# Local attention: queries and keys projected with features on partitions, instead of tokens and transposes

## The chip, the cores and the metric

The kernel runs on one core of a Trainium2 chip. The metric is the device time of one execution in microseconds; lower is better. The page of the profile and the trace come from one profiled execution. The engines are TensorE (PE, with PEld for its weight loads), VectorE (DVE), ScalarE (ACT), GpSimd (POOL) and SyncE (SP), which only issues transfers here. ACT and POOL have DMA queues of their own too.

## The reference

Input `x` is (4, 512, 256) in f32: four batches of 512 tokens. Three stages come first and are not touched by the change: a mixture of experts, a block attention with feature maps, and a second attention with a field term. Then two layers of a local transformer follow, each with its own weights:

```python
def _layer(x, wqkv, qs, ksc, wo, lg, lb, w1, b1, w2, b2):
    h = shift_token(x)                  # half of the features come from the token before
    q, k, v = jnp.split(h @ wqkv, 3, axis=-1)       # 8 heads of 64 each
    q = l2norm(q) * qs
    k = l2norm(k) * ksc
    q, k = rotary_xpos(q, k)
    ...                                 # local attention, @ wo, residual, feed forward

def l2norm(t):
    return t / jnp.clip(jnp.linalg.norm(t, axis=-1, keepdims=True), 1e-12)

def rotate_half(x):
    x1, x2 = jnp.split(x, 2, axis=-1)
    return jnp.concatenate([-x2, x1], axis=-1)

# in rotary_xpos:
q = q * cos * scale + rotate_half(q) * sin * scale
k = k * cos / scale + rotate_half(k) * sin / scale
```

Local attention has windows of 128 tokens: a query sees the keys of its own window and of the one before, up to 128 back, with a factor of 8 on the products. A key tile of 128 therefore meets 256 queries (128 at the end of the sequence). The feed forward normalizes, projects to twice 682 features, gates with gelu and projects back.

## The kernel before

The whole local transformer is in `local_stream`. `y[b]` holds a batch with tokens on partitions. The work of one layer is built of pieces for each batch.

`front(w, b, d)` makes queries, keys and values. It turns `y[b]` into `yT` with features on partitions (eight transposes into `pdt`, two copies). For each of four token tiles and each of queries and keys, `project` runs two 128x512 products with the tokens stationary, so that the result has tokens on partitions and all eight heads along its rows. ScalarE squares it (L614), VectorE sums the squares of each head (L615), multiplies by the table `tab` (L617) and multiplies the swapped halves by the second part of the table (L621, two instructions), and GpSimd adds the two (L624) into `qr`. A swap of halves is only another view along the row there. After all four tiles come a square root, a maximum and a reciprocal on the lengths `ss` (L628 to L630) and four value projections with copies (L633). Then the queries are multiplied by their lengths (L639), and 32 transposes into `pqt` (L82, through the helper) with copies (L646) give `qT` and `kT`, features on partitions. `mm` records every product at L78.

`scores(d, c, u)` takes a pair of heads `c` and a half `u` of the key tiles: products into `pds` with keys on partitions, Exp (L666, one instruction for each key tile, with the key's length as the scale), and a product with the mask `lmask` (L668). `values(l, b, d, c)` multiplies by the values (`pn`), and for every second `c` sums the exponentials with `ones32` (`pz`); the sums go through memory (SP's transfers L698 to L705: `sums`, `rden`, `rows`, `zb`) and come back spread over partitions for the product at L708. `tail` is the output projection `pdy`, `normed`, `turned`, `hidden` and `output` the feed forward; `turned` adds the last bias on GpSimd (L751).

What runs in which order on TensorE is written out by hand: inside `PE.in_order()` the products keep the order of the program. The loop over `k` goes through batches and head pairs; between `scores` and `values` it calls `spend`, which takes steps of a filler, `beside(b)`: steps of the next batch's `front`, then of the `tail` of the batch before.

```python
if b < B:
    scores(ds[b], c, 0)
spend(2 if b < B - 1 else 1)
if k > 0:
    b0, c0 = divmod(k - 1, 4)
    values(l, b0, ds[b0], c0)
spend(2 if b < B - 1 else 1)
if b < B:
    scores(ds[b], c, 1)
spend(2 if b < B - 1 else 1)
```

`first_two` prepares the fronts of batches 0 and 1 (`lead` runs ahead of the loop; in layer 1 it runs beside the end of layer 0's feed forward). The last batch's filler is the feed forward. The other engines' order comes from a scheduler that follows the program. The pool `lp` holds two buffers of a tag where nothing else is said; the feed forward's `u` tiles use the tags `kT` and `qT`.

Of the kernel before, what the change touches and what calls it, by code (L numbers as in the profile page):

```python
# [63 lines left out]
def adaln_attn_ffn_kernel(ctx: ExitStack, tc: tile.TileContext, a: dict, out: bass.AP):  # L64
# [115 lines left out]
    def row(name):  # L180
        return rows[name]
# [381 lines left out]
    def local_stream(dw, lp, y, dr):  # L563
        ones32 = dw.tile([128, 32], F32, tag="ones32", name="ones32")
        nc.gpsimd.memset(ones32, 1.0)

        def attn_weights(l):
            wqkv = weight("wqkv", [128, 2, 3 * DIN], a["f_wqkv"][l].rearrange("(c p) o -> p c o", p=128), dw)
            wo = weight("wo", [128, 4, H], a["f_wo"][l].rearrange("(c p) o -> p c o", p=128), dw)

            tab = weight("tab", [128, 4, NT, DHD], a["rot"], dw)
            for s, nm in enumerate(("qs", "ks")):
                sc = row(nm)[:, l * DHD : (l + 1) * DHD]
                nc.vector.tensor_tensor(
                    tab[:, 2 * s], tab[:, 2 * s], sc.unsqueeze(1).to_broadcast([128, NT, DHD]), ALU.mult)
                for d0, d1 in ((0, 32), (32, 0)):
                    nc.vector.tensor_tensor(
                        tab[:, 2 * s + 1, :, d0 : d0 + 32], tab[:, 2 * s + 1, :, d0 : d0 + 32],
                        sc[:, d1 : d1 + 32].unsqueeze(1).to_broadcast([128, NT, 32]), ALU.mult)
            return SimpleNamespace(wqkv=wqkv, wo=wo, tab=tab)  # L580

        def ffn_weights():
            return SimpleNamespace(w1=dw.tile([128, 2, 2 * HIDW], F32, tag="w1", name="w1"),
                                   w2=dw.tile([128, NU + 1, H], F32, tag="w2", name="w2"))

        def load_ffn(l, w):
            load(w.w1, a["f_w1"][l].rearrange("(c p) o -> p c o", p=128))
            load(w.w2, a["f_w2"][l].rearrange("(c p) o -> p c o", p=128))

        def front(w, b, d):  # L590

            yT = lp.tile([128, 2, S + 1], F32, tag="yT", name="yT", bufs=1)
            nc.gpsimd.memset(yT[:, 1, 0:1], 0.0)
            for c in range(2):
                pt = mmt("pdt")
                for k in range(NT):
                    PE.transpose(pt[:, k * 128 : (k + 1) * 128], y[b][:, k, c * 128 : (c + 1) * 128], ident)
                nc.scalar.copy(yT[:, c, 1 : S + 1], pt)
                yield

            def project(t, s):
                lhs = [yT[:, 0, 1 + t * 128 : 1 + (t + 1) * 128], yT[:, 1, t * 128 : (t + 1) * 128]]
                ps = mmt("pdq")
                mm(ps, [(lhs[c], w.wqkv[:, c, s * DIN : (s + 1) * DIN]) for c in range(2)])
                return ps.rearrange("p (h d) -> p h d", d=DHD)

            d.ss = ss = lp.tile([128, NT, 2, DH], F32, tag="ss", name="ss")
            qr = []
            for t in range(NT):
                qr_t = lp.tile([128, 2, DH, DHD], F32, tag="qr", name="qr", bufs=4)  # L610
                for s in range(2):
                    p3 = project(t, s)
                    sq = lp.tile([128, DH, DHD], F32, tag="tmp", name="sq", bufs=3)
                    nc.scalar.activation(sq, p3, AF.Square)  # L614
                    nc.vector.reduce_sum(ss[:, t, s, :], sq, axis=AX.X)  # L615
                    t1 = lp.tile([128, DH, DHD], F32, tag="t1", name="t1")
                    nc.vector.tensor_tensor(  # L617
                        t1, p3, w.tab[:, 2 * s, t, :].unsqueeze(1).to_broadcast([128, DH, DHD]), ALU.mult)
                    t2 = lp.tile([128, DH, DHD], F32, tag="tmp", name="t2", bufs=3)
                    for d0, d1 in ((0, 32), (32, 0)):  # L620
                        nc.vector.tensor_tensor(  # L621
                            t2[:, :, d0 : d0 + 32], p3[:, :, d1 : d1 + 32],
                            w.tab[:, 2 * s + 1, t, d0 : d0 + 32].unsqueeze(1).to_broadcast([128, DH, 32]), ALU.mult)
                    nc.gpsimd.tensor_tensor(qr_t[:, s], t1, t2, ALU.add)  # L624
                    yield
                qr.append(qr_t)

            nc.scalar.activation(ss, ss, AF.Sqrt)  # L628
            nc.vector.tensor_scalar_max(ss, ss, 1e-12)
            nc.vector.reciprocal(ss, ss)  # L630
            d.v = lp.tile([128, NT, DH, DHD], F32, tag="v", name="v")
            for t in range(NT):
                nc.scalar.copy(d.v[:, t], project(t, 2))  # L633
                yield

            d.kT = lp.tile([128, 4, S], F32, tag="kT", name="kT")
            d.qT = lp.tile([128, 4, S], F32, tag="qT", name="qT")
            for t in range(NT):
                nc.vector.tensor_tensor(  # L639
                    qr[t][:, 0], qr[t][:, 0], ss[:, t, 0].unsqueeze(2).to_broadcast([128, DH, DHD]), ALU.mult)  # L640
                for s, dst in enumerate((d.qT, d.kT)):
                    pt = mmt("pqt")
                    for c in range(4):
                        PE.transpose(pt[:, c * 128 : (c + 1) * 128],
                                     qr[t][:, s, 2 * c : 2 * c + 2, :].rearrange("p h d -> p (h d)"), ident)
                    nc.scalar.copy(dst[:, :, t * 128 : (t + 1) * 128], pt.rearrange("p (c q) -> p c q", q=128))  # L646
                    yield
# [3 lines left out]
        def scores(d, c, u):  # L651
            pss = [mmt("pds") for r in range(2)]
            n = 512 - 128 * u
            for jj in range(2):
                j = 2 * u + jj
                e = min((j + 2) * 128, S)
                for r in range(2):
                    rr = slice(64 * r, 64 * r + 64)
                    PE.matmul(pss[r][:, jj * 256 : jj * 256 + e - j * 128],
                              d.kT[rr, c, j * 128 : (j + 1) * 128], d.qT[rr, c, j * 128 : e],  # L660
                              start=True, stop=True)
            for r in range(2):
                p = lp.tile([128, n], F32, tag=f"p{u}", name="p", bufs=5)
                for jj in range(2):
                    at = slice(jj * 256, min(jj * 256 + 256, n))
                    nc.scalar.activation(p[:, at], pss[r][:, at], AF.Exp,  # L666
                                         scale=d.ss[:, 2 * u + jj, 1, 2 * c + r : 2 * c + r + 1])
                nc.vector.tensor_tensor(p[:, :n], p[:, :n], lmask[:, :n], ALU.mult)  # L668
                d.ps[c, u, r] = p
# [15 lines left out]
        def values(l, b, d, c):  # L685
# [17 lines left out]
            zb = lp.tile([128, 2, S], F32, tag="zb", name="zb", bufs=1)  # L703
# [37 lines left out]
        def turned(l, b, f):  # L741
            f.hT = lp.tile([128, 2, S], F32, tag="hT", name="hT")
            for c in range(2):
# [8 lines left out]
                y[b], y[b], row("fb2")[:, l * H : (l + 1) * H].unsqueeze(1).to_broadcast([128, NT, H]), ALU.add)  # L752
# [54 lines left out]
        def feed_forward(l, w):  # L807
# [3 lines left out]
            yield from turned(l, 0, fs[0])  # L811
            for b in range(B):
                for i, _ in enumerate(hidden(l, w, fs[b])):
                    yield b
                    if i == 0 and b + 1 < B:
                        normed(b + 1, fs[b + 1])
                if b + 1 < B:
                    yield from turned(l, b + 1, fs[b + 1])
                yield from output(l, w, b, fs[b])


        load_rows("drows", dw)
        lmask = dw.tile([128, 4 * WIN], F32, tag="lmask", name="lmask")
        nc.scalar.dma_start(lmask, a["kmask"])
        wf = ffn_weights()
# [6 lines left out]
        def first_two(w, ds):  # L832
            first, second = (front(w, b, ds[b]) for b in range(2))

            def lead():
                for _ in range(20):
                    next(first)
                    yield
                for _ in range(2):
                    next(second)  # L840
                    yield
                yield from first
# [4 lines left out]
        with PE.in_order():  # L847
            for l in range(2):
# [4 lines left out]
                def beside(b):  # L853
# [8 lines left out]
                    for _ in range(9 if b else 7):  # L862
# [11 lines left out]

                for k in range(4 * B + 1):
# [6 lines left out]
                    spend(2 if b < B - 1 else 1)  # L882
# [3 lines left out]
                    spend(2 if b < B - 1 else 1)  # L886
                    if b < B:
                        scores(ds[b], c, 1)
                    spend(2 if b < B - 1 else 1)
# [833 lines left out]
def _shape_constants():  # L1723
# [35 lines left out]
    for sc in (f(8.0) * scale, f(1.0) / scale):  # L1759
        c, s = cos * sc, sin * sc  # L1760
        parts += [np.concatenate([c, c], 1), np.concatenate([-s, s], 1)]
    rot = np.stack(parts).astype(f).reshape(4, NT, 128, DHD).transpose(2, 0, 1, 3)
    return {"mconst": mconst, "bmask": bmask, "hmask": hmask, "lmask": lmask, "kmask": kmask, "peT": peT, "rot": rot}
# [3 lines left out]
def _lay_out(n):  # L1767
# [6 lines left out]
    def rows_of(w):  # L1774
# [24 lines left out]

    cols = {  # L1800
# [22 lines left out]
        "f_w1": fw1.reshape(2, H, 2 * HIDW), "f_w2": fw2,  # L1823
# [21 lines left out]
```

## Time and profile before

| what | value |
|---|---|
| three runs | 1388.95, 1391.64, 1391.56 us; median 1391.56 |
| profiled execution | 1386.44 us, span 1384.7 us |
| mean granted TensorE clock | 0.991 |
| busy: PE, DVE, ACT, POOL | 1335.9, 653.3, 587.7, 232.8 us |
| local transformer, in the span | about 722 to 1384 us |
| transposes into `pqt` | 256, 33.9 us busy |
| `project` and value products | 384 records, 177.1 us busy |

The time of the profiled execution is its span and 1.7 us around it. Groups of instructions go by line, engine, operation and tile; after the bar come busy microseconds, mean nanoseconds of one, and the engine's idle time just ahead of them with what ended it. A f32 product shows as two records, a transpose as one. Windows give busy time of each engine in a stretch, and the granted clock.

### The profile page before, as it was taken

The page shows a single profiled execution, that of the slowest core. Times are in us where ns is not written, and L with a number is a line of the kernel's source. Part 1 is how long each engine was busy: PE and PEld are TensorE (multiplying, and loading weights), DVE is VectorE, ACT ScalarE, POOL GpSimd, SP SyncE. Part 2 cuts the span into 40 slices and gives each one's busy share as a digit, 9 for nine tenths or more (in the row PEclk, how much of TensorE's full clock was granted, in tenths as well). Part 3 has the DMA queues.
Part 4 walks back from the last instruction along what each step waited for, and adds up shares of the span by engine and source line. Part 5 has one row for each costly group of instructions (what it writes and reads, how often), then busy time and mean ns, then how long its engine had stood idle before and what let it go on. Part 6 is the DMA issues. An engine that isn't in the chain of part 4 may idle for free.

```text
span 1384.7 us, 19465 instructions
## 1 busy us (share of the span) xinstructions
PE 1335.9 (96%) x7632; PEld 827.5 (60%) x7632; DVE 653.3 (47%) x1295; ACT 587.7 (42%) x997; POOL 232.8 (17%) x223
## 2 busy tenths in 40 slices
PE   5999999998999999999999999999999999999998
PEld 4788888874566633333334555656555566556654
DVE  6222212224777643332227687654362777854421
ACT  4111111125555355454655756662223667474111
POOL 1325322211000011010104232100020322310110
PEclk7999999999999999999999999999999999999999
DMA  4577667633000000000210001210001010011000
GB/s 143 209 261 271 226 218 250 208 121 126 1 1 1 1 1 1 1 1 1 88 53 21 17 25 32 78 40 24 23 1 42 24 33 25 17 40 41 22 24 25
DMA packets 43085, 94.74 MB, mean 68 GB/s; under 512 B 9568, under 2 KB 25064, under 8 KB 40168
## 3 DMA queue, kind: packets, MB, share of 16 engines
q1 hardware_dynamic: 37560, 81.81, 17.8%
q0 software_dynamic: 3792, 10.24, 2.2%
q10 hardware_dynamic: 1632, 1.34, 0.3%
q8 instruction: 63, 1.03, 0.3%
q14 instruction: 38, 0.31, 0.1%
HBM read 84.08 MB, written 7.21 MB: 66 GB/s over the span
## 4 chain that ended last, share of the span: by engine, by line
PE 89%; DVE 5%; ACT 2%; DMA 2%; issue 1%; SPq 0%; DVEq 0%; POOLq 0%; POOL 0%; ACTq 0%
PE ph L78 14%; PE pdq L78 12%; PE pfy L78 6%; PE pug L78 5%; PE pv L78 5%; PE pua L78 5%; PE sc L78 5%; PE po L78 4%; PE pn L78 4%; PE pdy L78 4%; PE pds L78 4%; PE pz L78 2%; PE pqt L82 2%; PE pqk L78 1%; PE pf L78 1%
## 5 line engine op out<-in xcount | busy, mean ns | idle before, releaser
L78 PE MATMUL pdq<-wqkv,yT 128*128 128x512 f32 x384 | 177.1, 602 | 0.0
L416 ACT ACTIVATE cex<-sc 128x1024 f32<-128x1024 f32 x128 | 124.0, 1021 | 96.7 <-PE sc L78 95.9
L78 PE MATMUL ph<-h,w 128*128 128x256 f32 (+1 forms) x704 | 133.4, 347 | 0.5 <-ACT h L1398 0.5
L624 POOL TENSOR_TENSOR qr<-t,t 128x512 f32<-128x512 f32 x64 | 85.9, 1343 | 266.4 <-DVE t L621 221.7
L668 DVE TENSOR_TENSOR p<-p,lmask 128x384 f32<-128x384 f32 (+1 forms) x128 | 92.4, 736 | 68.4 <-ACT p L666 67.2
L78 PEld LDWEIGHTS ph<-h,w 128*128 128x128 f32 x704 | 116.1, 191 | 12.9 <-ACT h L1398 0.7
L78 PEld LDWEIGHTS pdq<-wqkv,yT 128*128 128x128 f32 x384 | 69.6, 190 | 78.1 <-issue 72.8
L1398 ACT ACTIVATE h<-ph,w 128x256 f32<-128x256 f32 (+1 forms) x88 | 35.4, 438 | 182.7 <-PE ph L78 130.1
L1400 DVE TENSOR_SCALAR h<-ph,w 128x256 f32<-128x256 f32 (+1 forms) x88 | 36.1, 438 | 162.4 <-PE ph L78 109.2
L666 ACT ACTIVATE p<-pds,ss 128x256 f32<-128x256 f32 (+1 forms) x256 | 96.1, 457 | 39.1 <-PE pds L78 30.6
L78 PE MATMUL pug<-hT,w 128*128 128x512 f32 x160 | 76.8, 602 | 0.0
L78 PE MATMUL sc<-qm,kT 32*128 32x512 f32 x512 | 75.2, 639 | 0.2 <-ACT cex L416 0.2
L78 PE MATMUL pua<-hT,w 128*128 128x512 f32 x160 | 75.2, 592 | 0.0
L614 ACT ACTIVATE sq<-pdq 128x512 f32<-128x512 f32 x64 | 38.3, 598 | 85.2 <-PE pdq L78 49.2
L78 PE MATMUL pv<-cex,v 128*32 128x512 f32 x512 | 69.0, 604 | 2.1 <-DVE xT L290 2.1
L78 PE MATMUL ph<-xbT,w 128*128 128x256 f32 (+1 forms) x352 | 68.5, 347 | 0.5 <-ACT xbT L123 0.5
L387 POOL TENSOR_SCALAR fterm<-vw,faT 128x256 f32<-128x256 f32 x16 | 14.6, 925 | 320.3 <-DVE cr L377 320.3
L78 PE MATMUL po<-w,h 128*128 128x256 f32 x296 | 67.7, 380 | 0.5 <-ACT h L1398 0.5
L78 PE MATMUL pds<-qT,kT 64*128 64x256 f32 (+1 forms) x512 | 65.3, 375 | 0.0
L78 PEld LDWEIGHTS pds<-qT,kT 64*128 64x128 f32 x512 | 43.9, 186 | 32.9 <-issue 25.8
L78 PEld LDWEIGHTS ph<-xbT,w 128*128 128x128 f32 x352 | 58.4, 191 | 7.7 <-issue 0.9
L78 PE MATMUL pdy<-wo,oT 128*128 128x256 f32 x256 | 61.5, 386 | 0.0
(301 smaller groups left out, 2129.9 us busy)
## 6 DMA issues: line engine op xcount, KB each, us to landing
w<-in_moe_w_dram SPq DMA_DIRECT2D x22, 1024.0 KB, 6.3
w<-in_moe_w_dram SPq DMA_DIRECT2D x22, 640.0 KB
w<-in_moe_w_dram SPq DMA_DIRECT2D x22, 516.0 KB, 3.8
zb<-rows SPq DMA_DIRECT2D x32, 256.0 KB, 4.0
g<-ys SPq DMA_DIRECT2D x6, 512.0 KB, 5.1
wqkv<-in_f_wqkv_dram SPq DMA_DIRECT2D x2, 1536.0 KB
w<-in_f_w_dram SPq DMA_DIRECT2D x2, 1408.0 KB, 6.1
out_dram<-yc SPq DMA_DIRECT2D x16, 128.0 KB, 1.8
```

Of the source, the lines that this page charges most:

```text
L78: cls._queue(nc.tensor.matmul(*args, **kw))
L82: cls._queue(nc.tensor.transpose(*args, **kw))
L387: nc.gpsimd.tensor_scalar_mul(fterm[:, t, :], vw, W["faT"][:, t, b : b + 1])
L416: nc.scalar.activation(ex, pss[j], AF.Exp, scale=CHD**-0.5)
L614: nc.scalar.activation(sq, p3, AF.Square)
L624: nc.gpsimd.tensor_tensor(qr_t[:, s], t1, t2, ALU.add)
L666: nc.scalar.activation(p[:, at], pss[r][:, at], AF.Exp, scale=d.ss[:, 2 * u + jj, 1, 2 * c + r : 2 * c + r + 1])
L668: nc.vector.tensor_tensor(p[:, :n], p[:, :n], lmask[:, :n], ALU.mult)
L1398: nc.scalar.activation(dst, src, AF.Relu, bias=bias)
L1400: nc.vector.tensor_scalar(dst, src, bias, 0.0, ALU.add, ALU.max)
```

## The change

Queries and keys are now projected with the weight slice stationary and `yT` moving, so that the products come out with features on partitions, two heads of 64 to each 128 (`piece`). Copies put them straight into `qT` and `kT`. The rotation's partner of a feature is now on another partition: for each two pieces four transfers on SP's queue copy 32 partitions each (128 KB) into `sw`. The q and k scales are a column (`qks`) in two three-operand products with a table that has features on partitions (`tab`, loaded once from `rotT`), and GpSimd adds in place. Lengths come from products with ones: `lengths` multiplies the squares by `heads32` (four 32x512 products into `pl`), and the sums go to memory on ScalarE's queue, back on GpSimd's queue as 128x64 for square root, maximum and reciprocal, to memory on GpSimd's queue and, spread over partitions, into `zb` by eight transfers on SP's queue (256 KB each). Four VectorE products apply them to both `qT` and `kT`, so Exp needs no scale and is one instruction for 512 or 384 columns. The transposes into `pqt`, the products on `tab` for each layer and the load of `drows` are gone; the bias of `turned` is loaded for each layer (`b2`).

The line numbers in the diff's new code are some 15 to 18 above those before. `front` has 14 steps instead of 22, and the filler's steps are dealt out by a table `share` instead of two or one at each place. In the new order of batch 0, the second front's keys' lengths stand after scores(1,0), and no step of a front stands between scores(1,1) and scores(3,1).

```diff
         def attn_weights(l):
...
-            tab = weight("tab", [128, 4, NT, DHD], a["rot"], dw)
...
+            return SimpleNamespace(wqkv=wqkv, wo=wo, l=l)
...
+            def piece(s, c):
+                at = s * DIN + c * 128
                 ps = mmt("pdq")
-                mm(ps, [(lhs[c], w.wqkv[:, c, s * DIN : (s + 1) * DIN]) for c in range(2)])
...
+                mm(ps, [(w.wqkv[:, 0, at : at + 128], yT[:, 0, 1 : S + 1]), (w.wqkv[:, 1, at : at + 128], yT[:, 1, 0:S])])
+                dst = (d.qT, d.kT)[s]
+                nc.scalar.copy(dst[:, c, :], ps)
+                if c % 2 == 0:
+                    return
+                dst = dst[:, c - 1 : c + 1, :]
+                sw = lp.tile([128, 2, S], F32, tag="sw", name="sw", bufs=3)
+                for g in range(4):
+                    nc.sync.dma_start(sw[32 * g : 32 * g + 32], dst[32 * (g ^ 1) : 32 * (g ^ 1) + 32])
+                sqs[s, c // 2] = lp.tile([128, 2, S], F32, tag="sq", name="sq")
+                nc.scalar.activation(sqs[s, c // 2], dst, AF.Square)
+                for i, t in enumerate((sw, dst)):
+                    at = 4 * w.l + 2 * (1 - i) + s
+                    nc.vector.scalar_tensor_tensor(
+                        t, t, qks[:, at : at + 1], tab[:, 2 * s + 1 - i, :].unsqueeze(1).to_broadcast([128, 2, S]),
+                        ALU.mult, ALU.mult)
+                nc.gpsimd.tensor_tensor(dst, dst, sw, ALU.add)
...
+            def lengths(s):
+                ps = mmt("pl")
+                for c in range(4):
+                    PE.matmul(ps[32 * c : 32 * c + 32, :], heads32, sqs[s, c // 2][:, c % 2, :], start=True, stop=True)
+                z = lp.tile([128, S], F32, tag="z", name="z", bufs=1)
+                nc.scalar.copy(z, ps)
+                nc.scalar.dma_start(sums[s * DH : (s + 1) * DH], z[0:128:16, :])
+
+            for s in range(2):
+                for c in range(4):
+                    piece(s, c)
+                    if s and c == 1:
+                        lengths(0)
                     yield
...
             for t in range(NT):
-                nc.scalar.copy(d.v[:, t], project(t, 2))
...
+                if t == 1:
+                    lengths(1)
+                    rl = lp.tile([128, 2 * DH * S // 128], F32, tag="rl", name="rl", bufs=1)
+                    nc.gpsimd.dma_start(rl, sums.rearrange("h q -> (h q)").rearrange("(p n) -> p n", p=128))
+                    nc.scalar.activation(rl, rl, AF.Sqrt)
+                    nc.vector.tensor_scalar_max(rl, rl, 1e-12)
+                    nc.vector.reciprocal(rl, rl)
+                    rows_ = dr.tile([2 * DH, S], F32, tag="lrows", name="lrows")
+                    nc.gpsimd.dma_start(rows_.rearrange("h q -> (h q)").rearrange("(p n) -> p n", p=128), rl)
+                    for c in (0, 2):
+                        for s, dst in enumerate((d.qT, d.kT)):
+                            zb = lp.tile([128, 2, S], F32, tag="zb", name="zb")
+                            for r in range(2):
+                                nc.sync.dma_start(
+                                    zb[64 * r : 64 * r + 64],
+                                    rows_.rearrange("(s c r) q -> s r c q", r=2, s=2)[s, r, c : c + 2].partition_broadcast(64))
+                            nc.vector.tensor_tensor(dst[:, c : c + 2, :], dst[:, c : c + 2, :], zb, ALU.mult)
                 yield
-
...
-                    pt = mmt("pqt")
-                    for c in range(4):
-                        PE.transpose(pt[:, c * 128 : (c + 1) * 128],
-                                     qr[t][:, s, 2 * c : 2 * c + 2, :].rearrange("p h d -> p (h d)"), ident)
-                    nc.scalar.copy(dst[:, :, t * 128 : (t + 1) * 128], pt.rearrange("p (c q) -> p c q", q=128))
...
-                    nc.scalar.activation(p[:, at], pss[r][:, at], AF.Exp,
-                                         scale=d.ss[:, 2 * u + jj, 1, 2 * c + r : 2 * c + r + 1])
+                nc.scalar.activation(p, pss[r][:, :n], AF.Exp)
...
-            zb = lp.tile([128, 2, S], F32, tag="zb", name="zb", bufs=1)
+            zb = lp.tile([128, 2, S], F32, tag="zb", name="zb")
...
             def lead():
...
+                yield from first
+                for _ in range(8):
                     next(second)
                     yield
...
-                    for _ in range(9 if b else 7):
+                    for _ in range(12 if b else 0):
...
+                more = ((2, 3, 2), (2, 2, 1), (1, 1, 1), (1, 1, 1))
+                share = (((1, 1, 1), (1, 0, 0)) + ((0, 0, 0),) * 2, more, more, ((1, 1, 1),) * 4, ((1, 1, 1),))
...
-                    spend(2 if b < B - 1 else 1)
+                    spend(share[b][c][0])
```

## The prediction

> **What bounds the kernel now.** I read the page's busy shares and chain first, then the windows over the stage that the change touches (722 to 1384 us), then groups, timelines and transfers for prices.
>
> ```profile
> PE 1335.9 (96%) x7632; PEld 827.5 (60%) x7632; DVE 653.3 (47%) x1295; ACT 587.7 (42%) x997; POOL 232.8 (17%) x223
> ...
> PE 89%; DVE 5%; ACT 2%; DMA 2%; issue 1%; SPq 0%; DVEq 0%; POOLq 0%; POOL 0%; ACTq 0%
> ```
>
> TensorE is the bound. A mean over stages can hide another limit, so the windows over the batches follow (PE is the second pair of numbers):
>
> ```profile
> 757.00:810.00 53.00, 53.00 (x324) 29.01 (x324) 39.08 (x75) 35.16 (x76) 15.82 (x13) 1.00 0.08 22
> 810.00:862.00 52.00, 51.84 (x312) 30.45 (x311) 40.30 (x85) 31.81 (x66) 13.43 (x10) 1.00 0.11 27
> ```
>
> PE is full in each batch, at a granted clock of 1.00. So PE work taken out is worth its whole time, and every wait that the new order lets through costs its whole time: there is no slack to absorb it. VectorE has 25% spare.
>
> **What PE loses and gains.** The groups by form (count, then busy us and mean ns):
>
> ```profile
> L78 PE MATMUL pdq<-wqkv,yT 128*128 128x512 f32 x384 | 177.1, 602 | 0.0
> L82 PE MATMUL pqt<-ident,qr 128*128 128x128 f32 x256 | 33.9, 277 | 0.8 <-DVE qr L639 0.8
> ```
>
> The projections keep count and shape (96 of 1.82 us on PE's queue); stationary and moving operand change places only: 0, since both are 128 x 128 slices against 512 columns. The 256 transposes go. What eight of them hold of PE's time is read from starts in the timeline:
>
> ```profile
> 1111.25 1.10 PE L82 MATMUL pqt<-ident,qr 128*128 128x128 f32 x8
> 1112.28 1.13 PE L78 MATMUL pds<-qT,kT 64*128 64x256 f32 x8
> 1113.34 1.09 PE L82 MATMUL pqt<-ident,qr 128*128 128x128 f32 x8
> 1114.37 1.73 PE L78 MATMUL pn<-p,v 128*64 128x256 f32 x16
> ```
>
> 1.03 us per eight beside other work, 0.94 in the opening (24 in 2.81): 28 x 1.03 + 4 x 0.94 = 32.6, and the wait of 0.8 ahead of them: **-33.4**. New are 16 length products, four 32x512 instructions each. The nearest row is the column-tiled `pv` of the earlier attention, same outputs:
>
> ```profile
> 700.11 1.06 PE L78 MATMUL pv<-cex,v 128*32 128x512 f32 x8
> 701.10 1.14 PE L78 MATMUL sc<-qm,kT 32*128 32x512 f32 x8
> ```
>
> A group's start to the next's is 0.99: 16 x 1.0 = **+16.0** (14 at the 0.87 of the cheapest eight in this stage, 22 at the 1.37 of the dearest `sc` group). PE work alone: **-17.4**.
>
> **Off PE.** VectorE per front: eight Squares' sums (0.68), eight table products (0.68), sixteen halves (0.41), four scalings (0.71) were 20.4 us. Now eight 128x1024 products of three operands and four with the broadcast lengths, at 1.22 of the nearest 128x1024 row (L1593): 14.7. ScalarE: 8 Squares of 0.60 and 8 copies of 0.62 become 8 copies and 4 Squares of about 1.0, the same; 256 Exps in 457 ns become 128 double ones, a little less. GpSimd: 8 adds of 1.34 become 4 of 2.44 (the 128x1024 add of L751) and two DMA issues. All lie under 53 us of PE: 0, and 2 to 5 us of a front each if that cover were gone. The tables' six products per layer and two loads go: off the path. SP gains 16 swaps and 8 broadcasts per front at 0.6 us of issue, 14.4 of 53 us, and some 4 MB. In its order the broadcasts of the next front stand ahead of the softmax sums of the batch under way (in batch 0, all of them), so a late length row holds those sums up. Their own chain took 11 us (sums issued 782.67, product 793.67) and the output projection stands some 25 us of PE work behind: 0, up to 3 per batch if SP is held over 14 us.
>
> **The new wait.** Scores now need the lengths, and these go PE, ScalarE, memory, GpSimd's queue, ScalarE, VectorE, GpSimd's queue, SP, VectorE. Transfers in the trace:
>
> ```profile
> zb<-rows SPq DMA_DIRECT2D x32, 256.0 KB, 4.0
> ...
> xb<-in_x_dram,rowtok POOLq DMA_INDIRECT x37, 4.4
> ...
> rden<-sums SPq DMA_DIRECT2D x16, 8.0 KB, 1.6
> ```
>
> Copy 0.6 (L633); sums to the next issue 1.8 (L698 to L699); small transfer on GpSimd's queue, between SP's 1.6 and the gather's 4.4, I take 3.0, the middle; Sqrt 0.3; max and reciprocal 1.1; second such transfer 3.0; two broadcast issues 1.3, landing 4.0, two more issues for the keys 1.3; product 1.2. Sum 17.6. Add a table load for Sqrt (1.28, as in the chain of before) and one VectorE pair held up, 2.07: **21.0**.
>
> By the Trainium skill's page "DMA: Bandwidth & Descriptors", section "Anatomy of one DMA — SWDGE (gpsimd) path", a transfer on that queue has about 2.0 us fixed; the chain would be 19 and the total about 10 lower (four batches 5, both batches 0 4, the opening 1.5). No direct small transfer on that queue is in this trace.
>
> Against it stands the PE work queued between the keys' length product and the scores:
> - Batches 1 and 2 of each layer: five score groups (1.06 or 0.85), four output projections and two value projections (1.82), two `pn` (1.67), one `pz` (1.65): 19.7. Short by 1.3, four times: **+5** (0 to 4 each).
> - Opening of layer 0, nothing else queued on VectorE: two value projections 3.6, eight transposes 1.0, six pieces 10.9, a product 1.0: 16.5, against 17.6 and 0.4 of the table load, the rest lying in the wait for the transfer: **+1.5** (0 to 8).
> - Batch 0 of each layer. The hand-made share gives nothing between scores and values from the second head pair on: after scores(1,1) only 1.06 us of PE work stand before values(1), and mask follows Exp 2.1 us after the scores end (scores until 1111.25, masks until 1113.38). So 1.0 is short. A mask caught under a GpSimd add is dearer:
>
> ```profile
> 816.00 1.26 POOL L624 TENSOR_TENSOR qr<-t,t 128x512 f32<-128x512 f32 x1 [1.02 <-DVE t L621]
> 816.08 2.07 DVE L668 TENSOR_TENSOR p<-p,lmask 128x384 f32<-128x384 f32 x2
> ```
>
>   That pair took 1.18 at 1112.20, so 0.9 more beside a 1.26 add; the new adds are twice as long, I take 1.3: 2.3. Before values(2) again 1.0, and the Sqrt, which ScalarE has between the two Exps of scores(2,0): 0.7. Then scores of batch 1: 15.0 us of queue and 4 of these stalls against 21.5: 2.5. **6.5 per layer, +13** (2 to 9 each).
> - Turn of the layers, where two pieces and a product stand last: **+1** (0 to 2.5).
>
> The Trainium skill's page "SBUF — State Buffer", section "Who interferes with whom", speaks against this change: VectorE with two inputs in SBUF and a GpSimd instruction that reads SBUF exclude each other for the whole instruction. The old rotation products read PSUM, the new ones read SBUF twice; by this rule a caught mask waits the whole 2.44 and batch 0 costs about 1 us more per catch than by my row.
>
> **Sum.** -33.4 + 16.0 + 5 + 1.5 + 13 + 1 = **+3.1**: the profiled execution (1386.44, span 1384.7) would go to 1389.5. That execution is 5.1 below the median of the runs, 1391.56, so I put the forecast on the median: **1394.7**. A difference of 0.2% (2.8 us) is about the least that can be told from no change.
>
> **Rivals.**
> 1. *Faster.* The waits are covered: transfers of about 2 us on GpSimd's queue, masks free. For it: PE idled 0.81 us in all on transposes before, ScalarE's Exps come in one piece. Against: the empty shares in batch 0 leave 1.0 twice per layer whatever the transfers do. -17.4 + 2 x 2 + 0.5 = -12.9: **1378.7**.
> 2. *Much slower.* GpSimd's queue takes the gather's 4.4 each way. The chain grows by 2.8 to 23.8: four batches +11.2, both batches 0 +5.6, opening +2.8; with the sum +22.7: **1414**. It decides from a chain of about 22 us. For it: the only waits of this kind in the trace are these 4.4 and 3.6; against: they gather or scatter, these are plain.
> 3. *No change that can be told*: stalls of 15 to 20 us against -17.4, **1389 to 1394**. The change not doing what it says is no rival: PE's written order of the changed kernel has no such transpose and sixteen length products.
>
> **Numbers.** Forecast case, slower by a little (own range 1394.4 to 1406): 0.40. Rival 1: 0.32, rival 2: 0.15, no change 0.13. So faster 0.32, same 0.13, slower 0.55. The range takes in both rivals' centres up to their outer halves: 1377 to 1413.
>
> **What would show it.** After: no `pqt` group; `pl` of 128 records near 0.6 us and 16 us on the path; PE busy down by about 17 and PE idle in the stage up by about 20, released by VectorE at `pn` (batch 0) and at `pds` (first scores of each batch), the latter traced to the broadcast lengths. Wrong if PE idle in the stage stays under 8 us (rival 1), if `pl` costs over 1.4 us a group, or if the transfers on GpSimd's queue take over 4 us (rival 2).

## The result

The changed kernel takes 1402.17 us (median of four runs) against 1390.26 for the kernel before in the same runs: 1.0087 times as long, interval 1.0073 to 1.0101. It is slower by 11.9 us; the forecast was slower by 3.1, with a range of 1377 to 1413.

The profiled execution has a span of 1400.5 us, 15.8 above the one of before. Of these, 4.1 lie ahead of the local transformer: its first transposes start at 725.30 us instead of 721.25, in stages that the change leaves alone. The rest, 11.7, lies in the local transformer, where the change is, and agrees with the 11.9 of the runs.

The page's busy times and the chain, after:

```profile
PE 1334.4 (95%) x7504; PEld 804.2 (57%) x7504; DVE 645.8 (46%) x1091; ACT 567.5 (41%) x852; POOL 239.5 (17%) x210
...
PE 80%; DVE 9%; DMA 5%; ACT 3%; issue 2%; SPq 1%; ACTq 0%; DVEq 0%; POOLq 0%; POOL 0%
```

TensorE's busy time fell by only 1.5 us, not by 17, and its share of the chain went from 89% to 80%: VectorE and transfers took over. The windows over the same stretches as before say where (PE is the second pair of numbers, the granted clock stands third from the end):

```profile
757.00:810.00 53.00, 46.82 (x280) 23.42 (x278) 34.84 (x37) 30.14 (x49) 16.96 (x8) 0.97 0.50 126
...
810.00:862.00 52.00, 51.87 (x303) 27.72 (x300) 39.04 (x61) 29.62 (x48) 12.11 (x8) 1.00 0.50 118
```

Batch 0 of layer 0 idles TensorE for 6.2 of 53 us; the next stretch is full again. The DMA share went from 0.08 and 0.11 to 0.50. VectorE's busy time in the first stretch even fell. So the idle time is not an engine that is full; it is who waits for whom. The waits of TensorE in the stage (total us, times, longest) name two:

```profile
PE pds L78 <- DVE kT L664: 7.6, 5, 3.3
PE pn L78 <- DVE p L683: 5.6, 4, 2.0
```

The first is the wait for the length products ahead of a batch's first scores, the second the wait for masks in the two batches 0. The groups of the projections and of the length products by form:

```profile
L78 PE MATMUL pdq<-yT,wqkv 128*128 128x512 f32 x256 | 119.4, 604 | 0.3 <-ACT yT L596 0.3
L78 PE MATMUL pdv<-wqkv,yT 128*128 128x512 f32 x128 | 61.6, 608 | 0.0
L78 PE MATMUL pl<-sq,heads 128*32 128x512 f32 x128 | 18.0, 605 | 0.0
```

One stretch of the timeline (774 to 800 us, batch 0 of layer 0) shows the waits on the masks and the chain of the lengths. The columns are start, duration, engine, line and instruction; in brackets the idle time before it and what ended that:

```profile
774.88 3.75 POOL L625 TENSOR_TENSOR qT<-qT,sw 128x1024 f32<-128x1024 f32 x1 [15.99 <-DVE qT L622]
...
776.34 3.38 DVE L622 SCALAR_TENSOR_TENSOR sw<-sw,qks,tab 128x1024 f32<-128x1024 f32 x1
776.75 0.55 ACTq L634 DMA_DIRECT2D lsums<-z  x1
...
779.03 0.55 POOL L651 DMA_DIRECT2D rl<-lsums  x1 [0.41 <-issue]
...
780.83 3.77 DVE L683 TENSOR_TENSOR p<-p,lmask 128x384 f32<-128x384 f32 x3
781.04 2.54 POOL L625 TENSOR_TENSOR qT<-qT,sw 128x1024 f32<-128x1024 f32 x1 [1.46 <-DVE qT L622]
781.43 0.65 PE L78 MATMUL pn<-p,v 128*64 128x256 f32 x2 [1.40 <-DVE p L683]
781.88 1.28 ACT L652 ACT_TABLE_LOAD   x1 [1.81 <-DMA rl<-lsums]
...
784.05 2.18 PE L78 MATMUL pn<-p,v 128*64 128x256 f32 x10 [1.97 <-DVE p L683]
...
784.74 0.55 DVE L654 RECIPROCAL rl<-rl 128x64 f32<-128x64 f32 x1
...
787.34 12.54 SPq L661 DMA_DIRECT2D zb<-lrows  x8
...
797.16 1.21 DVE L664 TENSOR_TENSOR kT<-kT,zb 128x1024 f32<-128x1024 f32 x1
...
798.51 1.14 PE L78 MATMUL pds<-qT,kT 64*128 64x256 f32 x8 [1.11 <-DVE kT L664]
```

The reader is to see three things. A rotation product that takes 1.27 us alone takes 3.38 beside a GpSimd add, and three masks take 3.77 (1.75 in the run below whose adds are not on GpSimd). TensorE waits twice for those masks. And the lengths' chain, from the end of TensorE's product at 776.1 to the end of VectorE's second length product at 798.4, takes 22.3 us; its hops stand in the queues of ScalarE, GpSimd, VectorE and SP, among their other work.

Just after the two mask waits the clock of TensorE halves for one stretch, whose window is:

```profile
784.30:787.70 3.40, 3.40 (x26) 1.74 (x26) 3.25 (x5) 1.42 (x2) 0.56 (x1) 0.50 0.03 10
```

3.4 us at 0.50 cost 1.7 us of work, by estimate (half of 3.4); it happens once more at 1132.4 us, after the wait of 3.26 us there. The Trainium skill's page "TensorE: Matmul & The Clock Gate", section "HAM oscillation — how this bites in real kernels", asks for no idle gaps over some 3.4 us. Here the half clock followed gaps of 1.4 and 2.0 us within five, so gaps shorter than that rule's can go with it. The length of one gap does not decide it in these runs: in the kernel of the first experiment below, a wait of 3.12 us, over at 1130.4 us, was followed by none:

```profile
1130.40:1137.20 6.80, 6.80 (x68) 4.26 (x69) 2.84 (x3) 3.33 (x6) 0.00 (x0) 1.00 0.62 144
```

### The profile page after: what moved, and what is told of

Its sections match the earlier page's. It is cut to its first block, busy times and chain, and to the rows that moved or that the text cites. A ratio compares the mean times of both kernels' runs of the same rounds, so it can differ in the third digit from the quotient of the medians.

```text
span 1400.5 us, 19183 instructions
## 1 busy us (share of the span) xinstructions
PE 1334.4 (95%) x7504; PEld 804.2 (57%) x7504; DVE 645.8 (46%) x1091; ACT 567.5 (41%) x852; POOL 239.5 (17%) x210
## 4 chain that ended last, share of the span: by engine, by line
PE 80%; DVE 9%; DMA 5%; ACT 3%; issue 2%; SPq 1%; ACTq 0%; DVEq 0%; POOLq 0%; POOL 0%
PE ph L78 14%; PE pdq L78 8%; PE pfy L78 6%; PE pv L78 5%; PE sc L78 5%; PE pug L78 5%; PE pua L78 5%; PE po L78 4%; PE pn L78 3%; PE pdy L78 3%; PE pdv L78 3%; PE pds L78 2%; DVE p L683 2%; PE pz L78 2%; PE pqk L78 1%
## 5 line engine op out<-in xcount | busy, mean ns | idle before, releaser
L78 PE MATMUL pdq<-yT,wqkv 128*128 128x512 f32 x256 | 119.4, 604 | 0.3 <-ACT yT L596 0.3
L683 DVE TENSOR_TENSOR p<-p,lmask 128x384 f32<-128x384 f32 (+1 forms) x128 | 96.3, 784 | 48.0 <-ACT p L682 47.8
L682 ACT ACTIVATE p<-pds 128x384 f32<-128x384 f32 (+1 forms) x128 | 64.1, 544 | 44.8 <-PE pds L78 37.8
L78 PEld LDWEIGHTS pdq<-yT,wqkv 128*128 128x128 f32 x256 | 45.8, 189 | 55.1 <-issue 51.3
L625 POOL TENSOR_TENSOR qT<-qT,sw 128x1024 f32<-128x1024 f32 x16 | 42.2, 2640 | 199.3 <-DVE qT L622 119.7
L78 PE MATMUL pn<-p,v 128*64 128x256 f32 (+1 forms) x512 | 59.9, 363 | 5.6 <-DVE p L683 5.6
```

The costliest lines, as they stand in the source:

```text
L78: cls._queue(nc.tensor.matmul(*args, **kw))
L625: nc.gpsimd.tensor_tensor(dst, dst, sw, ALU.add)
L682: nc.scalar.activation(p, pss[r][:, :n], AF.Exp)
```

## The experiments

Theory A at the start: the loss comes from GpSimd's adds, which hold up VectorE, and from the lengths' chain. The rivals: the swaps' transfers (B), and TensorE's own work with the empty shares in batch 0 (C).

**Adds on VectorE.** Edit:

```diff
-                nc.gpsimd.tensor_tensor(dst, dst, sw, ALU.add)
+                nc.vector.tensor_tensor(dst, dst, sw, ALU.add)
```

> The changed kernel with one edit: the four adds of the rotation per front run on VectorE instead of GpSimd. Theory A (the waits come from GpSimd's adds: they hold up masks and length products on VectorE, and the two transfers of the lengths queue behind them on GpSimd's queue): TensorE's waits on the masks (5.6 us) and on the lengths (7.6 us) lose more than half, one or both half-clock stretches in the stage (1.7 us each) go with them; 6 to 12 us below the changed kernel's 1402.2, so 1390 to 1396, although VectorE gets 32 more instructions of about 1.2 us. Rival B (the swaps' transfers and SP's queue set the pace): within 3 us of 1402. Rival C (TensorE's own work is what was mis-sized, the waits come from the empty shares): within 3 us of 1402, waits on masks unchanged.

Measured: 1397.0 us, 1.0050 times the kernel before (1.0037 to 1.0062), 5.2 below the changed kernel. The waits:

```profile
PE pds L78 <- DVE kT L664: 9.1, 3, 3.4
PE pn L78 <- DVE p L683: 1.7, 1, 1.7
```

The masks' waits fell from 5.6 to 1.7 us, so the adds were what held the masks in batch 0; C falls for them. The instructions agree: in the changed kernel nine masks beside a rotation's add took over 2 us, and here the only three over 1 us lie beside adds that GpSimd still has. The wait for the lengths did not fall (9.1), the time at half clock did not either (one stretch of 6.8 us instead of two of 3.4), and the gain stayed just under the expected 6 to 12. A holds for some 5 of the 12 us.

**No lengths.** The length products, their transfers and the products on VectorE are left out; Exp gets a fixed factor.

```diff
-                    if s and c == 1:
-                        lengths(0)
...
-                if t == 1:
-                    lengths(1)
...
-                nc.scalar.activation(p, pss[r][:, :n], AF.Exp)
+                nc.scalar.activation(p, pss[r][:, :n], AF.Exp, scale=1e-3)
```

> The changed kernel without the lengths: no products with ones, no transfers of sums and rows, no length products on VectorE; Exp takes a fixed factor of 0.001 instead, so queries and keys are not normalized. Swaps, rotation and GpSimd's adds stay. Theory A: the 17.0 us of length products go, the waits on the lengths (7.6) and their half-clock stretch (1.7) too, and the masks' waits stay in part: 26 to 30 us below the changed kernel, 1372 to 1376. Rival B: only the products go, as the swaps still fill SP's queue: 17 to 20 below, 1382 to 1385. Rival C: 17 below, as the waits then come from the shares.

Measured: 1370.67 us, 0.9858 (0.9833 to 0.9882), 31.5 below the changed kernel and 19 below the kernel before. So projecting with features down, with 128 swaps and all, is a gain; the lengths eat it and 12 us more. TensorE's idle time in the stage fell from 17.1 to 6.4 us, its work by 20.7, of which 17.0 are the products. A's 26 to 30 was a little exceeded; B's 17 to 20 and C's 17 fall.

**Length products twice.**

```diff
-                for c in range(4):
+                for c in (0, 1, 2, 3) * 2:
```

> The changed kernel with each length product issued twice (64 more 32x512 instructions of the same inputs and output). All theories that hold TensorE for the bound (A, and the forecast's term of 1.0 us each): 16 to 18 us above the changed kernel, 1418 to 1420. Rival D (a good part of the products lies in time in which TensorE would wait anyway): under 10 us above.

Measured: 1409.75 us, 1.0147 (1.0120 to 1.0174), only 7.6 above the changed kernel: rival D. The products' time on TensorE rose by 13.7, but its idle time fell from 17.1 to 11.7, so a good part of the added work lies in time in which TensorE waited anyway. The waits moved too (masks 8.6 us, lengths 2.1), so this is no clean price.

**No swaps.** The first product of the rotation reads the feature itself.

```diff
-                for g in range(4):
-                    nc.sync.dma_start(sw[32 * g : 32 * g + 32], dst[32 * (g ^ 1) : 32 * (g ^ 1) + 32])
...
-                        t, t, qks[:, at : at + 1], tab[:, 2 * s + 1 - i, :].unsqueeze(1).to_broadcast([128, 2, S]),
+                        t, dst, qks[:, at : at + 1], tab[:, 2 * s + 1 - i, :].unsqueeze(1).to_broadcast([128, 2, S]),
```

> The changed kernel without the 128 swap transfers: the first product of the rotation reads the feature itself instead of its partner, so the rotation is wrong, and the number and size of VectorE's and GpSimd's instructions is the same. Theory A: the masks are still caught under the adds, and the rotation comes some 4 us earlier: 0 to 4 us below the changed kernel, 1398 to 1402. Rival B: the waits on the lengths and masks go, 8 us or more below. Rival C: no change.

Measured: 1418.36 us, 1.0202 (1.0178 to 1.0226). Sixteen us slower with 128 transfers less: neither theory had this. The waits on the masks rose from 5.6 to 11.6 us and those on the lengths from 7.6 to 11.7. The timeline of the opening shows the reason for the longest (line numbers are two less in this kernel):

```profile
758.23 2.76 DVE L620 SCALAR_TENSOR_TENSOR sw<-qT,qks,tab 128x1024 f32<-128x1024 f32 x1 [0.76 <-ACT qT L611]
...
763.43 3.36 DVE L620 SCALAR_TENSOR_TENSOR sw<-kT,qks,tab 128x1024 f32<-128x1024 f32 x1
...
768.10 1.22 DVE L662 TENSOR_TENSOR kT<-kT,zb 128x1024 f32<-128x1024 f32 x1
...
769.47 0.80 PE L78 MATMUL pds<-qT,kT 64*128 64x256 f32 x2 [7.53 <-DVE kT L662]
```

The scheduler put the rotation of the second front, which has no transfer to wait for now, ahead of the length product that the first scores need, in VectorE's in-order queue; the rotation's products took 2.8 and 3.4 us beside GpSimd's adds, and TensorE waited 7.5 us. B's gain did not come, and a new suspicion rises: what decides is the order in the queues. It became rival E of the next runs.

**Earlier lengths.** If the chain is longer than the work queued behind it (theory A2), an earlier start must help.

```diff
-                if t == 1:
+                if t == 0:
                     lengths(1)
```

> The changed kernel with one edit: the keys' length product stands after the first value projection of a front instead of the second (1.82 us of TensorE's queue earlier). Theory A2 (the lengths' chain of some 22 us is longer than the work queued behind it, and everything that waits in a row behind VectorE's and GpSimd's queues adds to it): the waits on the lengths (7.6 us in the changed kernel) fall by up to 1.8 each in the four to five places, with one half-clock stretch: 4 to 8 us below 1402, 1394 to 1398. Rival C (the waits come from the empty shares around the masks): within 2 us of 1402, as the masks wait as before. Rival E (the scheduler's order on VectorE decides, and any edit reshuffles it): anywhere from 1395 to 1410, with the waits on the masks changed by over 3 us.

Measured: 1418.56 us, 1.0202 (1.0173 to 1.0230). A2 falls in this form: the waits on the lengths went only from 7.6 to 6.6. Of rival E the sign came true, the masks' waits, but not its time (up to 1410). The mask waits grew from 5.6 to 18.3 us, and the timeline of batch 0 shows why:

```profile
776.89 1.28 ACT L652 ACT_TABLE_LOAD   x1 [0.25 <-DMA rl<-lsums]
...
779.75 1.36 ACT L682 ACTIVATE p<-pds 128x384 f32<-128x384 f32 x3
...
782.07 3.77 DVE L683 TENSOR_TENSOR p<-p,lmask 128x384 f32<-128x384 f32 x3
...
782.68 0.65 PE L78 MATMUL pn<-p,v 128*64 128x256 f32 x2 [4.37 <-DVE p L683]
```

The root of the lengths, with a table load on either side, now stands ahead of the Exps on ScalarE; reciprocal and rotation stand ahead of the masks on VectorE, and the masks themselves lie beside a GpSimd add again (3.77 us for three). In this stretch the chain's own steps hold up the softmax.

**A new dealing of steps**, the same with the adds on VectorE, and that with bfloat16 length products. Edit of the first:

```diff
-                for _ in range(8):
+                for _ in range(11):
                     next(second)
...
-                more = ((2, 3, 2), (2, 2, 1), (1, 1, 1), (1, 1, 1))
-                share = (((1, 1, 1), (1, 0, 0)) + ((0, 0, 0),) * 2, more, more, ((1, 1, 1),) * 4, ((1, 1, 1),))
+                more = ((1, 2, 1), (2, 2, 1), (1, 1, 1), (1, 1, 1))
+                share = (((0, 0, 1),) * 3 + ((0, 0, 0),), more, more, ((1, 1, 1),) * 4, ((1, 1, 1),))
...
                         fill = beside(b)
+                        spend(4 if b else 0)
```

and the lengths after the first value projection, as above. The other two also have the adds on VectorE, and the third has `sq` and `heads32` in bfloat16.

> The changed kernel with its steps dealt out anew, nothing else: the lengths of the second front stand ahead of batch 0's first scores (11 steps in the lead instead of 8), its three other value projections fill the gaps between scores and values of batch 0, the keys' length product stands after the first value projection, and in batches 1 to 3 four steps of the next front (or feed forward) stand ahead of the first scores. TensorE then has about 20 us behind the lengths in batch 0 and 28 after, against a chain of 22. Theory A2: waits on the lengths under 2 us in all, waits on the masks under 3, no half-clock stretch: 12 to 18 us below 1402, 1384 to 1390, level with the kernel before or a little faster. Rival E: the masks still wait behind rotation work on VectorE: 1392 to 1400.

> The kernel of the new order with the rotation's adds on VectorE instead of GpSimd. Theory A (adds on GpSimd hold up masks and length products, and its queue holds up the lengths' transfers): another 2 to 6 us below the new order alone, 1380 to 1387. Theory A2 alone (once the cover is long enough, the chain's own length does not matter): within 2 us of the new order alone.

> The kernel of the new order with the adds on VectorE, and the squares and the ones of the length products in bfloat16 instead of f32 (sums still in f32). By the two records that each f32 product of the trace shows, a bfloat16 product has one at most: the 17 us of length products fall to 4 to 9: 8 to 13 us below the new order with adds on VectorE, 1370 to 1377, and below the kernel before. Rival: the products cost the change of tiles and the weight load, not the passes: under 4 us.

Measured: 1431.29 us, 1.0305 (1.0288 to 1.0322); 1420.29, 1.0224 (1.0200 to 1.0249); 1422.52, 1.0221 (1.0187 to 1.0256). The times missed all expectations, though moving the adds gave 11.0 us, more than the 2 to 6 expected of it. The masks' waits did fall, to 3.5 us in the first, but 4.2 us stayed at the lengths, and others took their place: 16.6 us at the output projection and 7.0 at the feed forward, as my steps ahead of batch 3's first scores draw the output projection of batch 2 forward, and it waited there for its softmax sums. And on SP a swap waited for one of its three buffers, with the lengths' broadcasts behind it:

```profile
771.19 14.64 SPq L617 DMA_DIRECT2D sw<-kT  x8
785.93 16.27 SPq L661 DMA_DIRECT2D zb<-lrows  x8
```

The bfloat16 products took 6.0 us of TensorE instead of 17.2, as expected, and the time did not follow: idle time rose from 29.6 to 37.5.

**Only batch 0 dealt anew**, with a fourth swap buffer, VectorE's adds and bfloat16; and **VectorE's adds and bfloat16 alone**, with the changed kernel's own steps. Edits: `range(8)` to `range(11)`, `(((1, 1, 1), (1, 0, 0)) + ((0, 0, 0),) * 2` to `(((0, 0, 1),) * 3 + ((0, 0, 0),)`, `bufs=3` to `bufs=4` of `sw`, and `t == 0`, for the first.

> The changed kernel with the adds on VectorE, squares and ones in bfloat16, a fourth buffer for the swapped halves (SP stood 14.6 us before a swap that waited for a buffer in the new order), and of the new order only the part at batch 0: 11 steps in the lead, the three other value projections in the gaps, the keys' length product after the first value projection; no step ahead of a batch's first scores. Theory E2 (what the engines' in-order queues hold up decides: the swaps' buffers on SP, the feed forward's and output projection's place in batch 3): waits of the new order at the output projection (7.7 and 7.5 us) and at the first scores (3.0) go, length products take 6 us instead of 17: 1378 to 1386, below the kernel before. Rival (earlier length products move the square root and the maximum ahead of masks, as in the kernel with only that edit): 1395 to 1410.

> The changed kernel with two edits: the rotation's adds on VectorE, squares and ones in bfloat16; its own dealing of steps. If TensorE's time saved on length products (11 us of 17) is worth its whole time: 1397.0 less 11, 1386. If half of it turns into waits, as half of the doubled products came out of waits: 1391 to 1393. Rival (the products' time was cover for the lengths' chain): no gain, 1396 to 1398.

Measured: 1397.41 us, 1.0067 (1.0049 to 1.0086), the rival's time but not its cause: the masks wait only 2.9 us, and the lengths 14.4, of which one wait is 10.0; and 1393.34, 1.0042 (1.0028 to 1.0057). The second looks like the middle case, but the kernel before took 1387.24 in these runs and 1389.80 in those of the adds on VectorE alone (1397.0). Each against its own kernel before, the two are 6.1 and 7.2 us slower, with intervals that overlap (1.0028 to 1.0057 and 1.0037 to 1.0062). So about 1 us came of the products' 11, which is nearest to the rival, no gain; the profiled executions give 2.0 in the stage (668.7 against 670.7). TensorE's length products fell by 11.3 us, but its idle time in the stage rose by 6.1 and its other work by 3.2:

```profile
PE pds L78 <- DVE kT L664: 13.3, 5, 5.3
```

**A shorter chain** on top of that:

```diff
-                    nc.scalar.activation(rl, rl, AF.Sqrt)
-                    nc.vector.tensor_scalar_max(rl, rl, 1e-12)
+                    nc.scalar.activation(rl, rl, AF.Sqrt, bias=tiny)
...
-                                nc.sync.dma_start(
+                                (nc.sync, nc.gpsimd)[s].dma_start(
```

> The changed kernel with the adds on VectorE and bfloat16 length products, and a shorter chain of lengths: the maximum goes (the root gets 1e-24 added instead), and the keys' four broadcasts go on GpSimd's queue beside the queries' four on SP's. The chain took 19 to 22 us with 1 to 4.6 us of it between reciprocal's and second product's turns on VectorE and the second pair of issues; it should take 16.5 to 18.5. Theory (waits are the chain's excess over the work behind it, each with a clock step): the waits at the first scores (13.3 us in the kernel without this edit) fall to 2 to 5, 1381 to 1387, level with the kernel before or up to 0.5% faster. Rival (any edit moves VectorE's order, and the waits come back in other places): 1389 to 1397.

Measured: 1403.97 us, 1.0092 (1.0077 to 1.0107), slower than even the rival said. The waits at the first scores fell from 13.3 to 8.1 us, not to 2 to 5. The chain did not get shorter (18.5 to 21.8 us, against 19.0 to 22.0): with the keys' broadcasts on GpSimd's queue, 6.3 to 8.7 us passed from their issue to the first product, against 5.1 to 8.1 before. New waits came at the feed forward (4.9 us).

**All of the lengths, but nobody waits.** Every instruction and transfer stays; only the result goes elsewhere.

```diff
-                            nc.vector.tensor_tensor(dst[:, c : c + 2, :], dst[:, c : c + 2, :], zb, ALU.mult)
+                            nc.vector.tensor_tensor(zb, dst[:, c : c + 2, :], zb, ALU.mult)
```

> The changed kernel with every instruction and transfer of the lengths kept, but the four products of a front write their result over the broadcast rows, so that no scores wait for them (queries and keys are not normalized, Exp takes a fixed factor of 0.001). What this gains against the changed kernel's 1402.2 is the price of the wait alone; what is left against the kernel without lengths (1370.7) is the price of TensorE's 16 products and of the queues. Theory: waits at the first scores 7.6 us and a half-clock stretch or two of 1.7 go: 1391 to 1394, and some 21 us above the kernel without lengths, of which 17 are the products. Rival (the wait draws the mask waits after it): 1384 to 1390. Rival (the scheduler's order moves, as in the other edits): over 1396.

Measured: 1405.99 us, 1.0109 (1.0085 to 1.0134): no gain at all. Not one wait for a length product is left, and the idle time in the stage is 17.1 us as before. It now lies at the masks (5.6), at the first scores of batch 1, which wait 2.6 us for the rotation's add on GpSimd, and at the feed forward of batch 0, which waits 5.9 us for its normalized rows (timeline of this kernel):

```profile
891.18 13.56 SPq L661 DMA_DIRECT2D zb<-lrows  x8
...
905.39 0.78 SPq L741 DMA_DIRECT2D hn<-yc  x1
...
909.42 1.23 DVE L664 TENSOR_TENSOR zb<-kT,zb 128x1024 f32<-128x1024 f32 x1 [2.68 <-DMA zb<-lrows]
...
913.36 1.92 PE L82 MATMUL pht<-ident,hn 128*128 128x128 f32 x4 [5.93 <-DVE hn L753]
```

The broadcasts of the lengths hold SP for 13.6 us, as the two buffers of `zb` come free only when VectorE gets to the products; the shifted rows of the feed forward's normalization queue behind them on SP, and its statistics behind the length products on VectorE.

What the experiments show is that the lengths as a whole cost 31 us, and the adds on GpSimd some 5. What the last three point to, and do not show by themselves, is that with the lengths in place the time is decided by what stands behind their steps in the in-order queues of ScalarE, VectorE, GpSimd and SP, more than by their result being late for the scores. Against the kernel without lengths (1370.67), the one in which nobody waits for them costs 35 us, of which 16.9 are products and 10.7 more idle time. Which single queue is the worst is not settled: every edit also moved the scheduler's order, and no run held that order fixed. No version here beats the kernel before; the kernel without lengths does, but it leaves out a part of the computation.

## Why the prediction was right or wrong

The side was right: slower, and a time inside the range. The size was not: 3.1 forecast, 11.9 measured. That the time still fell into the range is partly luck: TensorE's work came out 13.2 us above the forecast (-3.4 instead of -16.6) and the rise of its idle time 4.1 us below (15.6 instead of 19.7), so that two errors partly cancel, and the range was wide enough to hold both rivals. By its steps, with TensorE's time from the start of one group to the start of the next, read over the whole stage:

- **Transposes out**, -32.6 and a wait of 0.8: measured -31.4 and the wait gone. Right.
- **Length products**, +16.0: +17.0, one of them 1.0 late for its squares at the turn of the layers. Right.
- **All else on TensorE unchanged**, 0: this is the step that failed. The forecast had nothing for it, from the count and shape of the projections alone. The projections took 2.8 us more (175.1 against 172.2), the products with the values (`pn`) 3.3, the output projection 2.0, the turning of `yT` 1.0, the others 1.9: +10.9 in all. Two stretches at half clock are 3.4 of it, by estimate, none of it in the projections or the output projection; waits inside a group of products, which the list of waits does not show, are part (the `pn` at 790.27 us took 2.6 instead of 1.7). The lengths are not the cause of most of it: in the kernel without them, 7.3 of these 10.9 remain (projections 1.5, `pn` 3.6, output projection 1.6). Nor do the swaps' transfers explain the projections' part: without them the projections took 175.7, of which an estimated 1.0 is half clock. The projections lie in runs of four records oftener than before (48 instead of 20), and those runs took 0.46 us a record instead of 0.44, but nothing tests what that comes from; the cause of the projections' and the output projection's share stays open. So TensorE's work fell by 3.4 us, not by the forecast's 17.4 (16.6 of work and 0.8 of waiting).
- **Waits**, +20.5: idle time in the stage rose by 15.6, from 1.5 to 17.1. Batch 0: 10.0 visible against 13. First scores of batches 2 and 3: 1.7 against 5. (The cover of 19.7 reckoned there is the sum with four score groups, as the program has them, not with the five that the text names.) The opening: 2.0 against 1.5. Not foreseen: 3.0 at the feed forward and the output projection of batch 3.
- **The chain of the lengths**, 17.6 without and 21.0 with queueing: 17.9 to 22.3 in the eight fronts. Right as a sum, with two hops wrong that cancel: each small transfer on GpSimd's queue landed in 1.7 to 1.9 us (median, in the kernel with VectorE's adds and bfloat16), not 3.0, and the broadcasts took 5 to 9 us to the first product, not 5.3. For the transfers the Trainium skill's page "DMA: Bandwidth & Descriptors", section "Anatomy of one DMA — SWDGE (gpsimd) path", with its 2.0 us, was nearer than my middle of two rows.
- **SP's head of line**, 0 to 3: it was real (10.3 and 12.5 us of SP in the two batches 0), and in the changed kernel nothing late shows behind it; in the experiments it did.
- **The lock between VectorE and GpSimd**, taken at +1.3 per mask from a row: the adds on VectorE gave 5.2 us back. The Trainium skill's page "SBUF — State Buffer", section "Who interferes with whom", had the whole instruction blocked; nine masks that took over 2 us beside an add, instead of 0.55 to 0.68, agree with it better than with my +1.3.

Rival 1 (waits covered) fell with 17.1 us of idle time; rival 2 fell in its cause, as GpSimd's transfers were short, though the time lies half way to its number.

## What to carry to other kernels

Taking work off a full engine is worth its time only if what replaces it does not put a chain through the in-order queues of all the others: here 31 us of transposes went, and 17 us of products with a chain of some 20 us through three engines and three DMA queues cost 31. Even without that chain the change gave 19 us and not 31, as TensorE's other work and waits rose. Price such a chain not only by who waits for its end but by what stands behind each of its steps in every queue it passes (an Exp behind a root that waits for a transfer, a mask behind a maximum, a transfer behind a broadcast); the experiments point to this and do not price the queues one by one. And where a scheduler orders the queues, a small edit is not a small change: one step earlier cost 16 us. When versions come from different runs, compare each with the kernel before of its own runs: that turned an apparent 4 us here into 1.

## What was not expected of the hardware

TensorE's clock was at 0.50 for the 3.4 us that followed waits of 1.4 and 2.0 us within five, and again after one of 3.26, but not after one of 3.12 in another run; each such stretch costs an estimated 1.7 us on top of the wait. In bfloat16 the length products took 6 us instead of 17, a ratio of 2.9, not the two that the records of an f32 product suggest.
